# A graph attention layer on one core: GpSimd adds pairs of multiplied rows for VectorE

## Chip, core and metric

One core of a Trainium2 chip runs the whole kernel in one launch. The metric is device time in microseconds (us): the median of the runs shown.

## What is computed

A two-layer graph attention block on 10,000 nodes with 768 numbers each, and 170,000 edges, of which 10,000 are the nodes' own loops. Layer 1 has 4 heads of 256 numbers, layer 2 one head of 768. Cut to what matters here:

```
xl    = (x @ W).reshape(n, heads, out_ch)
e     = leaky_relu(alpha_src[src] + alpha_dst[dst], 0.2)
e     = exp(e - m[dst])                         # m: the largest e of each destination
alpha = e / (s[dst] + 1e-16)                    # s: the sum of e over each destination
msg   = xl[src] * alpha[:, :, None]
out   = segment_sum(msg, dst)                   # one sum of weighted rows for each node
```

The block adds a second edge list of loops to the one given; the kernel takes them in by doubling the weight of row 0. After each layer there is a layer norm and a residual product, and after layer 1 a relu; at the end the input is added and the whole is normalised once more.

## The kernel before

The work has three stages. The first multiplies all nodes by `W1`, writes the products and the attention terms as rows of 1,033 numbers into a table in DRAM, and sorts the nodes by their number of edges. The second is layer 1, the third layer 2. The change is in the second.

Layer 1 goes over 79 tiles of 128 nodes. A tile has as many *rows* as its nodes have edges at most (`SLOTS[t]`, 8 to 41): row k holds, in each partition, the table row of that node's k-th neighbour. The order of the tiles is such that the row counts climb from 8 to 41 and fall again to 9. GpSimd fetches each row by an indirect DMA (`gather`, L426) into a ring of 29 places in SBUF; the place of row k is fetched anew when row k has been used, for the row that comes 29 later. GpSimd works its queue in order, so a gather that waits holds up the next.

For each tile a sum of weighted rows is made in PSUM (`acc`, two of them in turn):

- Rows 0 to 3 (`on_pe`, 4 in every tile of 18 and more rows): ScalarE makes diagonal matrices of the weights (L725), TensorE multiplies and sums (L731).
- Of the others, every fourth (rows 4, 8, 12 and so on) is done by VectorE alone: four instructions that multiply one head and add it to `acc` (L531).
- The three between them are *shared*: ScalarE multiplies the row in place in the ring, one activation for each head (`multiply`, L520), and VectorE adds it to `acc` with one instruction over 1,024 numbers (L527). ScalarE's part is issued `LEAD` = 3 rows ahead (`multiplied(k + 1 + LEAD)`).

The program order within each engine is written out by hand; the loop `for k in range(n)` issues, for each row, ScalarE's multiplication of row k + 3, VectorE's work on row k, the gather into its place (`ring.fetch`), and whatever `due(k)` holds. Among these are the gather of the next tile's input (`next_x`, after row 6), the transposes of the tile before (hT, copied by ScalarE at L698), and its product for layer 2 (L879). Near the end of the loop, at row n - 3, VectorE makes the logits of the next tile (L489 and the lines behind it) from the attention terms in its rows, so these have to have landed by then. Then ScalarE makes the next diagonals. Before the next tile's row 4, VectorE does the layer norm of this one (L542 to L856).

Tiles of 22 and more rows are cut into two or three parts (`cuts_of`). The first part's weights are made ahead, as above; those of a later part are made within the loop (VectorE L489 to L496 and L765 to L773, ScalarE's diagonals L725 and the copy of TensorE's sum L778), and the sum so far is scaled when that part begins (L917).

```
def shared(t, k):
    return by_vector(t, k) and (k - on_pe(t)) % SHARE > 0
```

Of the kernel before, what the change touches and what calls it, by code (L numbers as in the profile page):

```python
# [51 lines left out]
SHARE = 4  # L52
ON_PE1 = 4
PARTED2 = 26
PARTED = 22


def chunk_counts(n_edges):
# [23 lines left out]
def gnn_kernel(ctx, tc, x, x_cols, src, dst, src_col, dst_col, W1, a_src1, a_dst1, b1, g1, be1, Wr1, br1,  # L82
               W2, a_src2, a_dst2, b2, g2, be2, Wr2, br2, out, n_edges):
    nc = tc.nc
# [3 lines left out]
    C1, C2 = H1 * DH1, H2 * DH2  # L88
# [8 lines left out]
    SLOTS = CAPS  # L97
# [3 lines left out]
    FIRST, TOTAL = [0] * NT, 0  # L101
# [414 lines left out]
    def multiply(row, e, dh):  # L516

        for h in range(e.shape[1]):
            s = slice(h * dh, (h + 1) * dh)
            nc.scalar.activation(row[:, s], row[:, s], AF.Copy, scale=e[:, h:h + 1])  # L520
# [13 lines left out]
    def pieces(a, width):  # L534

        return [a[:, c:c + width] for c in range(0, a.shape[1], width)]
# [106 lines left out]
    SLOTS, FIRST = [SLOTS[t] for t in TURNS], [FIRST[t] for t in TURNS]  # L643
# [4 lines left out]
    def begin_layer2(mem):  # L648


        rest = mem.shape[1]

        def at_end(n):
            nonlocal rest
            rest -= n
            return mem[:, rest:rest + n]

        firsts = [(at_end(C1), at_end(D0)) for _ in range(min(2, NT))]
        for t, (hT, xt) in enumerate(firsts):
            nc.sync.dma_start(hT, h1_d[turns[t]])  # L660
            nc.sync.dma_start(xt, x_d[turns[t]])
        wr2 = wr1.rearrange("p k n -> p (k n)")[:, :K1 * C2].rearrange("p (k n) -> p k n", n=C2)
        load(wr2, Wr2)
        br, ones = at_end(C2), at_end(P)
        yield
        nc.vector.memset(ones, 1.0)
        nc.vector.tensor_scalar(br, wr2[:, 0, :], br1_c[:, 0:1], None, op0=OP.mult)
        for k in range(1, K1):
            nc.vector.scalar_tensor_tensor(br, wr2[:, k, :], br1_c[:, k:k + 1], br, op0=OP.mult, op1=OP.add)
        yield wr2, firsts, br, ones, rest  # L670
# [4 lines left out]
    def ordered_layer1(mem):  # L675
        nc.scalar.add_instruction(mybir.InstLoadActFuncSet(name=nc.get_next_instruction_name(), act_func_set_id=6, engine=nc.scalar.engine))
        with tc.tile_pool(name="b1", bufs=1) as pool, tc.tile_pool(name="small1", bufs=2) as small, \
# [3 lines left out]
            ring = Ring(table1, RING1, {}, [mem.rearrange("p (k n) -> p k n", n=R1)])  # L681
# [30 lines left out]
            def on_pe(t):  # L712


                return min(max(SLOTS[t] // 2 - 5, 1), ON_PE1, SLOTS[t])

            def later_on_pe(t):

                return min(max((SLOTS[t] - 20) // 2, 1), ON_PE1)
# [61 lines left out]
            def cuts_of(t):  # L781

                n = SLOTS[t]
                groups = 1 if n < PARTED else -(-2 * n // ring.size)
                size = 8 if groups == 2 else (n - 5) // groups
                return [0] + [n - size * g for g in range(groups - 1, -1, -1)]

            def by_vector(t, k):
                lo = max(c for c in cuts_of(t)[:-1] if c <= k)
                return k - lo >= (later_on_pe(t) if lo else on_pe(t))  # L790

            def shared(t, k):
                return by_vector(t, k) and (k - on_pe(t)) % SHARE > 0
# [22 lines left out]
            for t in range(NT + 1):  # L816
                live, events = t < NT, []
                n = SLOTS[t] if live else 0
                first = done = on_pe(t) if live else 0
                cuts = cuts_of(t) if live else []  # L820
                if live and not ready:
                    ahead = weights_of(t)
                    ready += itertools.islice(ahead, 2)

                def row_of(k):
                    lo = max(c for c in es if c <= k)
                    return es[lo][0][:, k - lo], es[lo][1] if k == lo else None

                def multiplied(upto):
                    nonlocal done  # L830
                    while done < min(upto, n):
                        if shared(t, done):
                            multiply(ring.slot(FIRST[t] + done), row_of(done)[0], DH1)
                        done += 1

                if not live:
                    begin = begin_layer2(mem)
                    next(begin)
                later = iter(())
                if live:  # L840
                    es, acc = ready
                    es, later = dict(es), ahead
                if last:
                    r_before, means = last
                    stats = deviation(small, pieces(means[:, :C1], BANK))
                next(later, None)
                if full is not None:
                    store(t - 2)
                moves = []
                if live and t:  # L850
                    xT, moves = from_x(t)
                multiplied(first + 2)
                if last:
                    h = pool.tile([P, C1], F32, name="h")
                    scaled(h, [means[:, :C1]], stats, g1_b, be1_b)
                    nc.vector.scalar_tensor_tensor(h, h, 0.0, r_before[:, :C1], op0=OP.max, op1=OP.add)  # L856
                if not live:
                    begun = next(begin)
                for move in moves:
                    move()  # L860
                multiplied(first + LEAD)
                if last:
                    hT = pool.tile([P, K1, P], F32, name="hT")
                    events = [(first + j, move) for j, move in enumerate(halves(hT, h))]
                def by_wr1():
                    nonlocal r
                    if live and t:
                        r = product(xT, wr1, C1, ps_r)

                by_wr1()  # L870

                def to_layer2():
                    nonlocal full
                    nc.sync.dma_start(h1_d[t - 1], hT.rearrange("p k n -> p (k n)"))
                    full = []
                    for c in range(0, R2, BANK):
                        q = ps_half.tile([P, BANK], F32, name="half")[:, :min(BANK, R2 - c)]
                        for j in range(K1):
                            nc.tensor.matmul(q, hT[:, j, :], w2[:, j, c:c + q.shape[1]],  # L879
                                             start=(j == 0), stop=(j == K1 - 1))  # L880
                        full.append((c, q))

                if last:
                    events.append((cuts[1] - 2 * LEAD if len(cuts) > 2 else first + 2, to_layer2))

                def next_x():
                    nonlocal xt
                    xt = fetch_x(t + 1)

                if t and t + 1 < NT:  # L890
                    events.append((first + 2, next_x))
                events.sort(key=lambda event: event[0])

                def due(k):
                    while events and events[0][0] <= k:
                        events.pop(0)[1]()

                ready = []
                ahead = iter(())
                if live and t + 1 < NT:  # L900
                    ahead = weights_of(t + 1)
                for k in range(n):
                    if k + 2 * LEAD + 2 in cuts[1:-1]:
                        next(later)
                    if k + 2 * LEAD in cuts[1:-1]:
                        lo, es_lo = next(later)
                        es[lo] = es_lo
                    multiplied(k + 1 + LEAD)
                    if n - LEAD <= k < n - LEAD + 2:
                        ready += itertools.islice(ahead, 1)  # L910
                    if k + 2 in cuts[1:-1]:
                        next(later)
                    weights, fade = row_of(k)
                    if fade is not None:
                        for h in range(H1):
                            s = slice(h * DH1, (h + 1) * DH1)
                            nc.vector.scalar_tensor_tensor(acc[:, s], acc[:, s], fade[:, h:h + 1], ring.slot(FIRST[t] + k)[:, s],  # L917
                                                           op0=OP.mult, op1=OP.add)
                    if by_vector(t, k):
                        weigh(acc, ring.slot(FIRST[t] + k), weights, DH1, shared=shared(t, k))  # L920
                    ring.fetch(FIRST[t] + k + 1 + ring.size)
                    due(k)
                due(DEGREES)
                ready += itertools.islice(ahead, max(2 - len(ready), 0))
                last = None
                if live:
                    last = r, acc
# [459 lines left out]
```

## Time and profile before

| what | value |
|---|---|
| median of 14 runs | 5177.9 us (5174.55 to 5182.29) |
| the profiled execution | 5175.57 us, span 5173.8 us |
| VectorE (DVE) | 4280.8 us busy, 83% of the span |
| TensorE (PE) | 4761.2 us, 92% |
| ScalarE (ACT) | 2818.1 us, 54% |
| GpSimd (POOL) | 3289.0 us, 64% |
| 1500 to 2760 us, the tiles of 18 and more rows | VectorE 1134.70 us busy, TensorE 1135.25, ScalarE 1015.44, GpSimd 834.19 |

The profile names an instruction by its line, engine and operation, then `out<-in` by tile names. Times are microseconds unless marked as nanoseconds. "x12" is twelve instructions merged into one entry; "<-" in square brackets names what ended the idle time before an instruction. A busy TensorE need not be at its peak, since the ends of matmuls are modelled.

### The profile page before, as it was taken

To read this page: it belongs to the slowest core of one execution; us is meant where nothing else is said; L and a number is where in the kernel's file an instruction comes from. 1 tells how busy PE (TensorE), PEld (TensorE's weight loads), DVE (VectorE), ACT (ScalarE), POOL (GpSimd) and SP (SyncE) were. 2 spreads that over 40 slices of the span, in tenths; PEclk is the share of its full clock that TensorE was granted. 3 is DMA by queue.
4 is the path that set the end of the run, shared out by engine and by line. 5 is a ranking of instruction groups with operands and counts; after the bars stand their busy time and mean duration, and the time that the engine had idled before them with its cause. 6 is when DMAs were issued, how large, how long until landed. Compare 5 with 4: busy or idle time off the path is not lost. (4 is left out here: it accounts for less than half of the span.)

```text
span 5173.8 us, 60341 instructions
## 1 busy us (share of the span) xinstructions
PE 4761.2 (92%) x15307; PEld 2861.3 (55%) x15307; DVE 4280.8 (83%) x7678; ACT 2818.1 (54%) x8248; POOL 3289.0 (64%) x3429
## 2 busy tenths in 40 slices
PE   8999998899999988788999999999999999998875
PEld 3444443455555555555555555556666666665554
DVE  4785243899999888889999999789999898888887
ACT  3443433677778787887888777533333333333232
POOL 2445455656666666666666665277777777777774
PEclk9999999999999999999999999999999999999987
DMA  4333533999999999899999999599999999999996
GB/s 160 124 102 87 89 93 123 355 335 353 358 371 371 364 354 350 297 350 353 370 371 366 361 343 336 190 384 358 369 377 377 374 366 364 361 362 362 356 349 217
DMA packets 474312, 1591.43 MB, mean 308 GB/s; under 512 B 118327, under 2 KB 122487, under 8 KB 473958
## 3 DMA queue, kind: packets, MB, share of 16 engines
q0 software_dynamic: 322384, 1286.62, 67.7%
q1 hardware_dynamic: 149520, 297.43, 16.7%
q10 hardware_dynamic: 2054, 3.42, 0.2%
q8 instruction: 129, 2.11, 0.2%
q14 instruction: 225, 1.84, 0.1%
HBM read 1431.80 MB, written 177.29 MB: 311 GB/s over the span
## 5 line engine op out<-in xcount | busy, mean ns | idle before, releaser
L426 POOL DMA_INDIRECT ring<-table,slots x2675 | 2652.2, 991 | 1283.3 <-issue 317.1
L531 DVE SCALAR_TENSOR_TENSOR acc<-ring,e,acc 128x256 f32<-128x256 f32 (+1 forms) x2546 | 1586.5, 623 | 119.9 <-PE acc L731 44.7
L520 ACT ACTIVATE ring<-ring,e 128x256 f32<-128x256 f32 x3232 | 1320.5, 508 | 0.0
L527 DVE TENSOR_TENSOR acc<-acc,ring 128x1024 f32<-128x1024 f32 x808 | 994.9, 1231 | 72.7 <-ACT ring L520 5.6
L173 PE MATMUL big<-w,xT 128*128 128x512 f32 x1896 | 825.4, 597 | 22.9 <-DMA w<-in_W_dram 10.0
L879 PE MATMUL half<-w,hT 128*128 128x512 f32 (+1 forms) x2528 | 830.4, 486 | 0.0
L173 PE MATMUL big<-wr,xT 128*128 128x512 f32 x1896 | 829.5, 594 | 0.2 <-ACT xT L698 0.2
L1033 PE MATMUL big<-wr,w 128*128 128x512 f32 (+1 forms) x2464 | 819.7, 486 | 0.0
L988 PE MATMUL big<-ring,diagonals 128*128 128x256 f32 x2754 | 677.0, 408 | 130.6 <-ACT diagonals L987 111.9
L988 PEld LDWEIGHTS big<-ring,diagonals 128*128 128x128 f32 x2754 | 557.1, 205 | 247.9 <-ACT diagonals L987 149.2
L879 PEld LDWEIGHTS half<-w,hT 128*128 128x128 f32 x2528 | 477.8, 189 | 367.6 <-issue 309.0
L1033 PEld LDWEIGHTS big<-wr,w 128*128 128x128 f32 x2464 | 468.2, 190 | 326.4 <-issue 294.7
L173 PEld LDWEIGHTS big<-w,xT 128*128 128x128 f32 x1896 | 362.0, 192 | 482.0 <-issue 463.6
L731 PE MATMUL acc<-ring,diagonals 128*128 128x256 f32 x2056 | 509.7, 405 | 129.0 <-ACT diagonals L725 120.8
L173 PEld LDWEIGHTS big<-wr,xT 128*128 128x128 f32 x1896 | 355.2, 191 | 417.9 <-issue 417.2
L731 PEld LDWEIGHTS acc<-ring,diagonals 128*128 128x128 f32 x2056 | 411.7, 203 | 223.2 <-ACT diagonals L725 149.5
L987 ACT ACTIVATE diagonals<-ident,e 128x128 f32<-128x128 f32 x1377 | 411.2, 387 | 162.6 <-DVE e L511 134.0
L546 ACT ACTIVATE sd<-mv,eps 128x1 f32<-128x1 f32 x237 | 69.5, 293 | 753.8 <-DVE mv L544 753.7
L630 DVE TENSOR_TENSOR scr<-big,ad_b 128x1024 f32<-128x1024 f32 x79 | 96.7, 1224 | 376.6 <-ACT row L627 376.6
L725 ACT ACTIVATE diagonals<-ident,e 128x128 f32<-128x128 f32 x1028 | 315.2, 388 | 166.3 <-DVE e L511 145.2
L635 POOL TENSOR_TENSOR row<-row,none 128x1024 f32<-128x1024 f32 x79 | 187.1, 2368 | 262.7 <-ACT row L627 262.2
L497 ACT ACTIVATE e<-e 128x32 f32<-128x32 f32 (+26 forms) x174 | 41.1, 236 | 544.2 <-DVE e L496 518.8
(185 smaller groups left out, 3646.9 us busy)
## 6 DMA issues: line engine op xcount, KB each, us to landing
ring<-table,slots POOLq DMA_INDIRECT x2675, 7.0
table<-row SPq DMA_DIRECT2D x79, 516.0 KB, 3.6
h_d<-hT SPq DMA_DIRECT2D x79, 512.0 KB, 6.8
w<-h_d SPq DMA_DIRECT2D x77, 512.0 KB, 8.5
table<-row SPq DMA_DIRECT2D x79, 385.0 KB, 6.0
ring<-table SPq DMA_DIRECT2D x79, 385.0 KB, 6.4
xT<-in_x_cols_dram SPq DMA_DIRECT2D x79, 384.0 KB, 4.4
x_d<-xt SPq DMA_DIRECT2D x79, 384.0 KB, 6.6
```

The source lines that it names most:

```text
L173: nc.tensor.matmul(p[:, c:e], aT[:, j, :], w[:, j, c:e], start=(j == 0), stop=(j == k - 1))
L426: nc.gpsimd.indirect_dma_start(out=to, out_offset=None, in_=table, in_offset=bass.IndirectOffsetOnAxis(ap=index, axis=0), **more)
L520: nc.scalar.activation(row[:, s], row[:, s], AF.Copy, scale=e[:, h:h + 1])
L527: nc.vector.tensor_add(acc[:, :c], acc[:, :c], row[:, :c])
L531: nc.vector.scalar_tensor_tensor(acc[:, s], row[:, s], e[:, h:h + 1], (acc if first is None else first)[:, s], op0=OP.mult, op1=OP.add)
L635: nc.gpsimd.tensor_add(row[:, :C1], row[:, :C1], b1_b)
L725: nc.scalar.activation(diagonals[:, k * H1 + i, :], ident, AF.Copy, scale=e[:, k, i:i + 1])
L731: nc.tensor.matmul(acc[:, c:d], diagonals[:, k * H1 + i, :], ring.slot(q + k)[:, c:d], start=(k == 0 and c % BANK == 0), stop=(k == m - 1 ...
L879: nc.tensor.matmul(q, hT[:, j, :], w2[:, j, c:c + q.shape[1]], start=(j == 0), stop=(j == K1 - 1))
L987: nc.scalar.activation(diagonals[:, (k - lo) % G, :], ident, AF.Copy, scale=e[:, k - lo, :])
L988: nc.tensor.matmul(to, diagonals[:, (k - lo) % G, :], ring.slot(at + k)[:, ON_PE2:C2], start=False, stop=(k == n - 1), skip_group_check=True)
L1033: nc.tensor.matmul(r[:, c:d], hT[:, j, :], wr2[:, j, c:d], start=False, stop=(j == K1 - 1 and d < C2), skip_group_check=True)
```

## The change

In tiles of 18 and more rows (36 of the 79), at row 8 of the loop and ahead of row 8's own gather, GpSimd gets an instruction that adds row 10 to row 11 in place; both are shared rows that ScalarE has multiplied. VectorE's add of row 10 to `acc` is left out, and its add of row 11 takes the sum of the two. No instruction of TensorE, ScalarE or the DMA queue on SyncE is added or removed.

```diff
+PAIRED = 18
...
+            def paired(t):
+
+                return SLOTS[t] >= PAIRED
...
+                    if paired(t) and k == first + SHARE:
+                        one, two = (ring.slot(FIRST[t] + first + SHARE + j)[:, :C1] for j in (2, 3))
+                        nc.gpsimd.tensor_add(two, two, one)
                     weights, fade = row_of(k)
                     if fade is not None:
...
-                    if by_vector(t, k):
+                    if by_vector(t, k) and not (paired(t) and k == first + SHARE + 2):
                         weigh(acc, ring.slot(FIRST[t] + k), weights, DH1, shared=shared(t, k))
                     ring.fetch(FIRST[t] + k + 1 + ring.size)
                     due(k)
```

Here `first` is 4 and `SHARE` is 4.

## Prediction

> **What bounds the kernel now.** I read the page first, then the stretch that holds the 36 paired tiles and VectorE's waits in it, then single tiles in order of time. From the page, the add on each engine (busy us, mean ns | idle before it, and what ended most of it):
>
> ```profile
> L527 DVE TENSOR_TENSOR acc<-acc,ring 128x1024 f32<-128x1024 f32 x808 | 994.9, 1231 | 72.7 <-ACT ring L520 5.6
> L635 POOL TENSOR_TENSOR row<-row,none 128x1024 f32<-128x1024 f32 x79 | 187.1, 2368 | 262.7 <-ACT row L627 262.2
> ```
>
> The same add of 1,024 numbers a partition takes VectorE 1.23 us and GpSimd 2.37. The paired tiles run from 1500 to 2760 us; first their busy times (in the order PE, PE loads, DVE, ACT, POOL, then clock, DMA share, GB/s), then what VectorE waited for:
>
> ```profile
> 1500.00:2760.00 1260.00, 1135.25 (x3818) 701.99 (x3819) 1134.70 (x1814) 1015.44 (x2744) 834.19 (x936) 0.96 0.96 355
> ```
> ```profile
> DVE acc L531 <- PE acc L731: 29.5, 35, 2.3
> DVE acc L527 <- ACT ring L520: 5.1, 5, 1.9
> DVE e L489 <- DMA ring<-table,slots: 4.4, 10, 1.2
> ```
>
> VectorE is busy for 1,135 of 1,260 us and its three largest waits come to 39; the rest is small gaps between its instructions. It sets the pace. TensorE is as busy, but the page puts 120.8 us of idle time before its sums (L731) down to ScalarE's diagonals, so it follows: these come from ScalarE, whose factors come from VectorE's logits near the end of the tile before. DMA is busy too (0.96), yet VectorE waited for rows for only 4.4 us. So 1.23 us taken from VectorE in each tile should count, and so should every new wait of VectorE. What matters is when the sum of rows 10 and 11 is there. A tile of 18 rows, VectorE, ScalarE and GpSimd one after the other:
>
> ```profile
> 1535.12 2.06 DVE L531 SCALAR_TENSOR_TENSOR acc<-ring,e,acc 128x256 f32<-128x256 f32 x4
> 1537.28 3.91 DVE L527 TENSOR_TENSOR acc<-acc,ring 128x1024 f32<-128x1024 f32 x3
> 1541.23 2.06 DVE L531 SCALAR_TENSOR_TENSOR acc<-ring,e,acc 128x256 f32<-128x256 f32 x4
> ```
> ```profile
> 1533.40 1.06 ACT L698 COPY hT<-half 128x512 f32<-128x512 f32 x2
> 1534.34 4.92 ACT L520 ACTIVATE ring<-ring,e 128x256 f32<-128x256 f32 x12
> ```
> ```profile
> 1536.58 0.99 POOL L426 DMA_INDIRECT ring<-table,slots  x1 [0.30 <-issue]
> 1537.87 0.99 POOL L426 DMA_INDIRECT ring<-table,slots  x1 [0.30 <-issue]
> ```
>
> VectorE's three entries are row 8, rows 9 to 11, and row 12. ScalarE's 12 are rows 9, 10 and 11, four heads each (the view ends there): row 11 is multiplied at 1534.34 + 4.92 = 1539.26, after row 9's add has ended (1537.28 + 3.91 / 3 = 1538.6). ScalarE works without a pause here and is ahead of VectorE by only half a row. GpSimd's two are the gathers into the places of rows 7 and 8; the new add stands between them.
>
> **The change, part by part.** *Removed*: 36 adds on VectorE, row 10 of each paired tile, 1.23 us and a gap of 0.1 each: 36 x 1.34 = 48 us off the engine that sets the pace, if nothing takes their place.
>
> *Added*: 36 adds on GpSimd. Each waits for ScalarE's row 11. How soon an engine starts after that, and whether GpSimd's add is slowed by VectorE beside it, is seen in the first stage:
>
> ```profile
> 453.37 1.01 ACT L627 COPY row<-big 128x1024 f32<-128x1024 f32 x1 [5.56 <-issue]
> 454.42 1.22 DVE L630 TENSOR_TENSOR scr<-big,ad_b 128x1024 f32<-128x1024 f32 x1 [4.32 <-ACT row L627]
> 454.47 2.37 POOL L635 TENSOR_TENSOR row<-row,none 128x1024 f32<-128x1024 f32 x1 [1.30 <-ACT row L627]
> ```
>
> GpSimd starts 0.08 us after ScalarE's end (453.37 + 1.01 = 454.38, then 454.47), and takes its usual 2.37 beside a VectorE operation with one operand in PSUM and one in SBUF, which is what rows 8 and 9 are. So in the 18-row tile: the gather before the add ends at 1537.57 and does not bind; the add runs from 1539.34 to 1541.71. VectorE is through with row 9 at 1538.6 and stands for 3.2 us, since row 11 now needs GpSimd. Row 11 then runs from 1541.79 (0.08 again, an estimate from the same row) to 1543.02, where it ended at 1541.19. **The tile is 1.83 us longer, not 1.34 shorter.** Behind the waiting row 11 on VectorE stand rows 12 to 17, the next tile's logits and the layer norm; ScalarE's next diagonals, TensorE's next sums and VectorE's row 4 of the next tile follow from these, so the loss is carried on in full.
>
> I read the same times in each of the 36 tiles. The 24 tiles of 18 to 21 rows: 1.80 to 1.84 in 22 of them, 1.45 in two; together 43.0 us. Four tiles of 22 rows, cut in two parts: 1.30 to 1.38, together 5.4:
>
> ```profile
> 1933.14 1.28 ACT L725 ACTIVATE diagonals<-ident,e 128x128 f32<-128x128 f32 x4
> 1934.31 4.90 ACT L520 ACTIVATE ring<-ring,e 128x256 f32<-128x256 f32 x12
> ```
> ```profile
> 1934.51 3.91 DVE L527 TENSOR_TENSOR acc<-acc,ring 128x1024 f32<-128x1024 f32 x3
> ```
>
> There the diagonals of the second part come first, row 11 is the first of the 12 (4.90 / 3 = 1.63, so 1935.95), and the add ends at 1938.4 against row 9's end at 1935.8. In the eight tiles of 23 and more rows VectorE does the second part's weights between these rows, which covers most of the wait: -0.4 to +2.2, together 4.0. Sum: 43.0 + 5.4 + 4.0 = **+52.4 us**.
>
> *Moved*: on GpSimd's queue the gathers into the places of rows 8 to 11 stand behind the add. In the 18-row tile row 8's is issued at 1542.0 and not at 1537.87: 4.1 later, 2.3 later than VectorE itself has become. Who needs these rows? With a ring of 29, a tile of 18 rows that follows needs none of them before its own last logits were read; in tiles of 19 to 21 the next tile's logits read rows that were gathered just here. An example of 21 rows, row 12's gather and the logits that read it:
>
> ```profile
> 1830.84 0.99 POOL L426 DMA_INDIRECT ring<-table,slots  x1 [0.81 <-DVE acc L531]
> ```
> ```profile
> 1838.27 0.30 DVE L489 TENSOR_TENSOR e<-ring 128x84 f32<-128x84 f32 x1 [0.25 <-DMA ring<-table,slots]
> ```
>
> No slack is left there: the row lands 7.4 us after its issue, and VectorE waits 0.25. The bounds: at worst 17 tiles of 19 to 21 rows x 2.3 = 39 us; at best nothing, because a gather lands 2.1 to 10.5 us after its issue in this stretch (median 7.3), so that part of it is queueing, which a pause of 4 us on the issuing side lets run down. A gain from later gathers is excluded, since nothing starts sooner. I take 8, nearer to nothing, as the queueing above the shortest landing (7.3 - 2.1 = 5.2) is more than the 2.3. GpSimd's own time has room: 834 + 36 x 2.37 = 919 us of busy time in 1,260.
>
> What could lengthen the add is VectorE beside it. The Trainium skill (SBUF — State Buffer, "Who interferes with whom") says that a VectorE instruction with two SBUF inputs contends with a GpSimd instruction that reads SBUF, and that the one that comes second waits out the first. No run shown here has that pair; rows 8 and 9 have one operand in PSUM, so by it only the small weight operations of the eight long tiles could meet the add, at most about 1 us each by an estimate, and the sum would be some 8 us more.
>
> Sum: 52.4 + 8 = 60. The profiled execution took 5175.6 (span 5173.8), so its like would take 5236; the median of the 14 runs lies 2.3 higher at 5177.9, which gives **5238 us**.
>
> **Rivals.** *The gathers come late* (slower still): the same wait, with the 39 in place of the 8: 5178 + 52 + 39 = 5269. For it speaks that the logits of 19 to 21 rows have no slack; against it that a queue empties in a pause.
>
> *The saved add comes out* (faster): VectorE loses 1.34 us a tile and waits for nothing, 5178 - 48 = 5130. It decides at the point where GpSimd's add ends before row 9 does; in the 18-row tile it would have to start by 1538.6 - 2.4 = 1536.2, and ScalarE's row 11 would have to be 3.1 us earlier than it is. ScalarE has no pause in which to catch that up. Even an add that begins as soon as GpSimd is free (1537.6) ends at 1540.0 and brings 0.1 us a tile, or 5174. Three of the long tiles come out faster, by 0.4 at most.
>
> *Something hides the wait* (no change): VectorE already waits 29.5 us for TensorE's first rows, and if those waits were TensorE's own lateness they would shrink by as much; that leaves 52.4 - 29.5 = +23, or 5201, still slower. To reach no change nearly all of the wait must lie beside something else, and nothing of that size is idle on VectorE.
>
> *The change does nothing* is excluded: in the instruction order VectorE has one add fewer and GpSimd one more in each of 36 tiles, and VectorE's row 11 waits for GpSimd in place of ScalarE.
>
> **How the numbers follow.** Forecast, with up to 8 around its terms: 0.80; late gathers 0.11; faster 0.04; wait hidden 0.05, most of it at +23. A difference under 0.2% (10 us) can hardly be told from none here. Faster 0.04, same 0.03, slower 0.93. The range: below, the forecast without the gathers' 8, and half of the 29.5 hidden (5178 + 52 - 15 = 5215); above, the late gathers' 5269 and a little for a GpSimd add that is slower on these rows (0.1 us on 28 tiles is 3): 5272.
>
> **What would show it.** Right: VectorE's row 11 shows a wait for the new GpSimd add of about 3 us in 24 tiles, some 90 us in all; GpSimd's add lasts 2.4 and is released by ScalarE; tile periods of 18 rows grow from 29.8 to 31.6. Wrong: logits that wait for DMA by more than 40 us in all (then the late gathers), an add well over 2.4 us (then contention), or row 11 released by ScalarE or by nothing (then the faster case).

## The result, and the profile after

The changed kernel takes 5240.38 us (median of 6 runs, 5237.59 to 5244.67), the kernel before 5177.24 (28 runs). The ratio is 1.0122, with a 95% interval of 1.0112 to 1.0132: 63 us slower. The profiled execution has a span of 5241.3 us, 67.5 more than before. Lines of code have moved: L426 is now L427, L520 is L521, L527 is L528, L531 is L532, L731 is L736, and the new add is L920.

From the page after, VectorE's add and GpSimd's gathers:

```profile
L427 POOL DMA_INDIRECT ring<-table,slots x2675 | 2646.0, 989 | 1212.1 <-issue 337.1
L528 DVE TENSOR_TENSOR acc<-acc,ring 128x1024 f32<-128x1024 f32 x772 | 950.5, 1231 | 160.7 <-POOL ring L920 94.0
```

The 36 adds are gone (808 to 772, 44 us less busy), and 94.0 us of waiting for the new add stand in their place. The same stretch as before, now up to 2822 us, and VectorE's waits in it:

```profile
1500.00:2822.00 1322.00, 1154.57 (x3826) 718.13 (x3825) 1098.50 (x1775) 1015.65 (x2742) 914.66 (x969) 0.94 0.94 338
```
```profile
DVE acc L528 <- POOL ring L920: 90.8, 30, 3.6
DVE acc L532 <- PE acc L736: 41.0, 36, 2.7
DVE acc L528 <- ACT ring L521: 7.1, 9, 1.9
DVE e L490 <- DMA ring<-table,slots: 4.3, 8, 1.4
```

Two waits have grown by much: that for GpSimd from nothing to 91 us, and row 4's for TensorE from 29.5 to 41.0. The logits' wait for rows has not (4.4 before). The same 18-row tile as before the change, VectorE and then GpSimd, in order of time:

```profile
1539.90 2.06 DVE L532 SCALAR_TENSOR_TENSOR acc<-ring,e,acc 128x256 f32<-128x256 f32 x4
1542.07 1.23 DVE L528 TENSOR_TENSOR acc<-acc,ring 128x1024 f32<-128x1024 f32 x1
1546.51 1.23 DVE L528 TENSOR_TENSOR acc<-acc,ring 128x1024 f32<-128x1024 f32 x1 [3.21 <-POOL ring L920]
```
```profile
1541.37 0.99 POOL L427 DMA_INDIRECT ring<-table,slots  x1 [0.30 <-issue]
1544.12 2.36 POOL L920 TENSOR_TENSOR ring<-ring 128x1024 f32<-128x1024 f32 x1 [1.76 <-ACT ring L521]
1546.63 1.00 POOL L427 DMA_INDIRECT ring<-table,slots  x1 [0.15 <-issue]
```

Row 8, row 9, a wait of 3.21 us, row 11. GpSimd is free at 1542.36, waits 1.76 us for ScalarE's row 11, and adds for 2.36; VectorE goes on 0.03 us after its end. From the start of row 8 to the end of row 11 the tile is 1.77 us longer than before.

Below, *the stretch* is the time from VectorE's row 4 in the first 18-row tile to its row 4 in the first tile behind the paired ones (tile 22 to tile 58 by turn), as the starts in each trace give it: 1274.5 us before, 1339.1 after, 64.6 more.

### The profile page after: what moved, and what is told of

The parts are those of the page before. It is cut to its first block, busy times and chain, and to the rows that moved or that the text cites. A ratio compares the mean times of both kernels' runs of the same rounds, so it can differ in the third digit from the quotient of the medians.

```text
span 5241.3 us, 60307 instructions
## 1 busy us (share of the span) xinstructions
PE 4788.8 (91%) x15307; PEld 2881.4 (55%) x15307; DVE 4246.8 (81%) x7642; ACT 2819.7 (54%) x8248; POOL 3370.6 (64%) x3465
## 3 DMA queue, kind: packets, MB, share of 16 engines
q10 hardware_dynamic: 2054, 3.42, 0.2%
## 5 line engine op out<-in xcount | busy, mean ns | idle before, releaser
L427 POOL DMA_INDIRECT ring<-table,slots x2675 | 2646.0, 989 | 1212.1 <-issue 337.1
L532 DVE SCALAR_TENSOR_TENSOR acc<-ring,e,acc 128x256 f32<-128x256 f32 (+1 forms) x2546 | 1586.5, 623 | 132.1 <-PE acc L736 56.9
L521 ACT ACTIVATE ring<-ring,e 128x256 f32<-128x256 f32 x3232 | 1320.2, 507 | 0.0
L528 DVE TENSOR_TENSOR acc<-acc,ring 128x1024 f32<-128x1024 f32 x772 | 950.5, 1231 | 160.7 <-POOL ring L920 94.0
L736 PE MATMUL acc<-ring,diagonals 128*128 128x256 f32 x2056 | 530.0, 417 | 172.4 <-ACT diagonals L730 143.2
L736 PEld LDWEIGHTS acc<-ring,diagonals 128*128 128x128 f32 x2056 | 427.1, 211 | 271.9 <-ACT diagonals L730 168.2
```

The costliest lines, as they stand in the source:

```text
L427: nc.gpsimd.indirect_dma_start(out=to, out_offset=None, in_=table, in_offset=bass.IndirectOffsetOnAxis(ap=index, axis=0), **more)
L528: nc.vector.tensor_add(acc[:, :c], acc[:, :c], row[:, :c])
L532: nc.vector.scalar_tensor_tensor(acc[:, s], row[:, s], e[:, h:h + 1], (acc if first is None else first)[:, s], op0=OP.mult, op1=OP.add)
L736: nc.tensor.matmul(acc[:, c:d], diagonals[:, k * H1 + i, :], ring.slot(q + k)[:, c:d], start=(k == 0 and c % BANK == 0), stop=(k == m - 1 ...
```

## The experiments

The first eight runs fell on two other chips, on which the kernel before takes 5543 and 5547 us; the changed kernel's traces show where most of that comes from: 1862 us from row 4 of the last tile of layer 1 to the end on the first chip, 2216 on one of these two, but 1339 and 1345 for the stretch. So each run's ratio is to the kernel before on its own chip. The last four ran where it takes 5184. The stretches of the first eight runs have no trace of the kernel before from the same chip beside them, and their one tile of 41 rows took 65 to 73 us where the other traces have 64 to 65; they can be set beside the 1274.5 only to within some 8 us.

| run | ratio to the kernel before, 95% interval | stretch, us |
|---|---|---|
| changed kernel, first chip | 1.0122 (1.0112 to 1.0132) | 1339.1 |
| r1_after_again | 1.0118 (1.0101 to 1.0135) | 1344.7 |
| e1_no_add | 0.9977 (0.9962 to 0.9991) | 1266.2 |
| e2_idle_add, e2b_idle_add | 1.0067 (1.0046 to 1.0087), 1.0054 (1.0037 to 1.0071) | 1318.9, 1316.0 |
| e3_late_take | 1.0082 (1.0064 to 1.0100) | 1314.7 |
| e4_half | 1.0004 (0.9993 to 1.0016) | 1284.6 |
| e5_after_fillers | 1.0087 (1.0066 to 1.0107) | 1333.9 |
| e6_before_fillers | 0.9979 (0.9964 to 0.9994) | 1282.7 |
| r2_before_again | one run, 5188.68 us | 1273.8 |
| e8_fewer_fillers | 0.9991 (0.9982 to 1.0000) | 1266.8 |
| e9_idle_end | 1.0045 (1.0030 to 1.0061) | 1297.5 |
| e10_half_fillers | 0.9994 (0.9985 to 1.0003) | 1271.7 |

**The changed kernel again** (r1_after_again).

> The changed kernel as it is, so that the other runs of this call stand beside it on the same chip. Expected: about 1.012 times the kernel before, as measured first, if the loss is VectorE's wait for GpSimd's add (A), since that wait is set by ScalarE and GpSimd alone. If the loss hangs on when rows land (B), it differs on a chip whose rows land later.

1.0118, the same ratio within the intervals, on a chip whose layer 2 is some 350 us slower. VectorE's wait for GpSimd is again 90.9 us and the logits wait for DMA for 5.9. The loss does not hang on the chip.

**No add at all** (e1_no_add), against the changed kernel:

```diff
-                        nc.gpsimd.tensor_add(two, two, one)
+                        pass
```

> VectorE leaves out row 10 in the 36 tiles and GpSimd adds nothing, so the weighted sums lack row 10. If VectorE alone sets the pace (A), the time falls by 36 x 1.34 = 48 us from the kernel before, to about 5130. If TensorE or the arrival of rows is close behind (B), less comes out: the waits of VectorE's row 4 for TensorE grow and the fall is half or less, 5155 to 5178.

The fall is 12 us (5 to 21 by the interval), not 48 (5530.73 against 5542.73). Tiles of 18 rows, 29.8 us long before, mostly take 29.78. TensorE in one of them, in order of time:

```profile
1542.99 0.82 PE L698 MATMUL half<-ident,xt 128*128 128x128 f32 x6
1544.27 1.09 PE L698 MATMUL half<-ident,h 128*128 128x128 f32 x8 [0.46 <-ACT xT L699]
1545.20 10.47 PE L174 MATMUL big<-wr,xT 128*128 128x512 f32 x24
1555.50 10.51 PE L884 MATMUL half<-w,hT 128*128 128x512 f32 x32
1565.85 7.09 PE L736 MATMUL acc<-ring,diagonals 128*128 128x256 f32 x32
1572.77 0.82 PE L698 MATMUL half<-ident,xt 128*128 128x128 f32 x6
```

Each entry follows on the one before but for 0.46 us: here TensorE has no more time to give. VectorE's row 4 behind these sums waits 1.33 us for them, where it waited 0.66. ScalarE takes its part too. Rows 9 and 11 on VectorE in the same tile, and its waits for ScalarE in the stretch (5.1 us before the change):

```profile
1551.48 1.23 DVE L528 TENSOR_TENSOR acc<-acc,ring 128x1024 f32<-128x1024 f32 x1
1553.45 1.23 DVE L528 TENSOR_TENSOR acc<-acc,ring 128x1024 f32<-128x1024 f32 x1 [0.74 <-ACT ring L521]
```
```profile
DVE acc L528 <- ACT ring L521: 21.4, 24, 6.8
```

Row 11 now comes before ScalarE has multiplied it, so from row 8 to row 11 the 24 tiles of 18 to 21 rows gain 0.7 us each and not 1.34. Even a GpSimd add that cost nothing would have brought about a quarter of what the sum of VectorE's time says.

**An idle add** (e2_idle_add and e2b_idle_add, the same kernel twice), against the changed kernel:

```diff
-                        nc.gpsimd.tensor_add(two, two, one)
+                        idle = pool.tile([P, DH1], F32, name="idle")
+                        for c in range(0, C1, DH1):
+                            nc.gpsimd.tensor_add(idle, two[:, c:c + DH1], one[:, c:c + DH1])
...
-                    if by_vector(t, k) and not (paired(t) and k == first + SHARE + 2):
+                    if by_vector(t, k):
```

> GpSimd makes the same sum at the same place, in four pieces of 256 columns and into a scratch tile that nobody reads; VectorE adds rows 10 and 11 itself as before. If the loss is VectorE's wait for the sum (A), the time is that of the kernel before, 5177 to 5183. If it comes from the gathers that stand behind the add on GpSimd's queue (B), most of it is still there: 5205 or more, with VectorE's logits waiting for DMA.

> The idle add once more, to see whether its +37 us hangs on the chip. By (A) alone it should cost nothing: 0 to +6 us against the kernel before. By (B) it costs 25 us or more and VectorE's logits wait for DMA by 15 us or more in the 36 tiles.

Both came out at half of the whole loss, 37 and 34 us, though VectorE waits for nothing of GpSimd's. What it waits for in the second of them, and GpSimd's groups:

```profile
DVE acc L532 <- PE acc L736: 28.8, 31, 2.5
DVE e L490 <- DMA ring<-table,slots: 19.6, 14, 3.8
```
```profile
L427 POOL DMA_INDIRECT ring<-table,slots x757 | 771.5, 1019 | 321.2 <-issue 186.8 <-DVE acc L532 36.2 <-PE acc L736 31.6
L922 POOL TENSOR_TENSOR idle<-ring 128x256 f32<-128x256 f32 x140 | 102.4, 731 | 19.9 <-issue 6.6 <-ACT ring L521 4.1 <-ACT diagonals L730 0.5
```

The logits wait for rows that were gathered late. In the second run tiles of 18 rows mostly still take 29.8 us; those of 19 and 20 go from 31.2 to 33.2 and from 34.2 to 37.3 in the worst cases, against the first trace of before. GpSimd's gathers wait for themselves ("issue", 187 us against 76 before) and seldom for VectorE (36 against 109 for that line): the queue has become the slow one.

**The sum taken later** (e3_late_take), against the changed kernel; the gathers into places 11 to 13 are issued together after row 13:

```diff
-                    if by_vector(t, k) and not (paired(t) and k == first + SHARE + 2):
+                    if by_vector(t, k) and not (paired(t) and k in (first + SHARE + 2, first + SHARE + 3)):
...
+                    if paired(t) and k == first + SHARE + 5:
+                        weigh(acc, two, weights, DH1, shared=True)
-                    ring.fetch(FIRST[t] + k + 1 + ring.size)
+                    if not (paired(t) and first + SHARE + 3 <= k < first + SHARE + 5):
+                        ring.fetch(FIRST[t] + k + 1 + ring.size)
```

> GpSimd's add stays where it is; VectorE takes the sum after row 13 in place of row 11's turn, so that rows 12 and 13 (2.16 + 1.34 us) lie beside the add, and the gathers into places 11 to 13 follow then. If the place where VectorE takes the sum is what costs (A), VectorE's wait for GpSimd goes below 10 us in all and the time is under that of the kernel before, 5135 to 5165. If the queue behind the add costs (B), the logits of tiles of 19 to 21 rows wait for DMA and the time stays above it, 5185 or more.

VectorE's wait for GpSimd is gone (0.2 us in one case), as was expected; the gain is not. Its waits:

```profile
DVE e L490 <- DMA ring<-table,slots: 37.9, 14, 4.3
DVE acc L532 <- PE acc L736: 33.7, 28, 4.0
```

Late gathers have taken the place of the wait, and a loss of 0.82% is left of 1.18%. Part of this is the edit's own, since it holds the gathers into places 11 and 12 until row 13; how much was not measured. This gives (B) its due: the place where VectorE takes the sum sets what VectorE waits for, not whether it waits.

**The idle add at the end of the tile** (e9_idle_end), against the kernel before:

```diff
                     due(k)
+                    if n >= PAIRED and k == n - 1:
+                        idle = pool.tile([P, DH1], F32, name="idle")
+                        for c in range(0, C1, DH1):
+                            nc.gpsimd.tensor_add(idle, g1_b[:, c:c + DH1], be1_b[:, c:c + DH1])
```

> The idle add of four pieces at the end of each of the 36 tiles, behind the gather of the last row, on constants, so that it waits for nothing. If the idle add cost time by its place, ahead of the gathers into the places of rows 8 to 11 (B), it costs 0 to 8 us here. If it costs by the time that it takes from GpSimd (E), it costs about as much as before, 25 us or more.

It costs 21 us (1.0045), less than (E) expected and more than (B), with no wait in it and nothing but the next gathers behind it. So time taken from GpSimd costs something at this place too. The logits wait for DMA for 19.1 us again. How much of the earlier 34 to 37 us was the place this run does not tell, since its pieces are slower than those were. One tile's pieces on GpSimd, with VectorE's layer norm beside them:

```profile
1752.69 4.04 POOL L927 TENSOR_TENSOR idle<-g,be 128x256 f32<-128x256 f32 x4
1756.87 1.01 POOL L427 DMA_INDIRECT ring<-table,slots  x1
1758.19 1.00 POOL L427 DMA_INDIRECT ring<-table,slots  x1 [0.31 <-PE half L698]
```
```profile
1752.55 1.28 DVE L557 SCALAR_TENSOR_TENSOR h<-acc,mv,g 128x1024 f32<-128x1024 f32 x1
1753.93 1.40 DVE L559 SCALAR_TENSOR_TENSOR h<-h,sd,be 128x1024 f32<-128x1024 f32 x1
1755.44 1.22 DVE L857 SCALAR_TENSOR_TENSOR h<-h,big 128x1024 f32<-128x1024 f32 x1
```

Gathers follow at 1.3 us from one another behind that, 0.30 of it idle. The four pieces take 4.04 us. Three of them last 0.73 to 0.75 us each; the third, which began while L559 ran, lasts 1.59. One such long piece stands in 35 of the 36 tiles. L559 is slower as well, 53.5 us over the stretch against 47.6 for the same line before, so up to 6 of the 21 us are VectorE's own.

**Half an add** (e4_half), against the changed kernel:

```diff
-                        nc.gpsimd.tensor_add(two, two, one)
+                        nc.gpsimd.tensor_add(two[:, :C1 // 2], two[:, :C1 // 2], one[:, :C1 // 2])
...
-                    if by_vector(t, k) and not (paired(t) and k == first + SHARE + 2):
+                    if paired(t) and k == first + SHARE + 2:
+                        nc.vector.tensor_add(acc[:, C1 // 2:C1], acc[:, C1 // 2:C1], one[:, C1 // 2:])
+                    elif by_vector(t, k):
```

> GpSimd adds 512 of the 1,024 columns, VectorE adds the other half of row 10 itself. By A the add is about 1.2 us long (half of 2.36, an estimate) and ends 1.2 us earlier, so a tile of 18 to 21 rows loses 0.6 us and not 1.8: 24 x 0.6 = 14, the long tiles about nothing, in all 5187 to 5197. If an add on GpSimd has a fixed cost or the loss does not hang on its length (B), the time stays above 5215.

The whole loss is gone: 1.0004, better than the 10 to 20 us that were expected by (A). The add takes 1.27 us, and VectorE waits 12.7 us in all for it. An 18-row tile:

```profile
1555.33 1.23 DVE L528 TENSOR_TENSOR acc<-acc,ring 128x1024 f32<-128x1024 f32 x1
1556.67 0.70 DVE L928 TENSOR_TENSOR acc<-acc,ring 128x512 f32<-128x512 f32 x1
1557.93 1.23 DVE L528 TENSOR_TENSOR acc<-acc,ring 128x1024 f32<-128x1024 f32 x1 [0.56 <-POOL ring L920]
```

Row 9 ends at 1556.56 and row 11 begins 1.37 us later; before the change it began 1.44 later. The estimate took ScalarE to end row 11 some 0.7 us after VectorE's row 9, as it did before. In this tile GpSimd's half add began at 1556.62, so ScalarE was through just as row 9 ended: the shift of the engines against each other is not fixed (why it moved was not followed further), and the tile (29.78 us) is TensorE's.

**Fillers for TensorE.** Why does row 4 wait longer for TensorE after the change? A 20-row tile's first sums, before and after (TensorE in order of time):

```profile
2520.50 3.73 PE L731 MATMUL acc<-ring,diagonals 128*128 128x256 f32 x16 [1.43 <-ACT diagonals L725]
```
```profile
2568.95 10.17 PE L736 MATMUL acc<-ring,diagonals 128*128 128x256 f32 x32 [3.25 <-issue]
```

Before, sixteen in 3.73 us behind an idle time of 1.43 (the other sixteen follow, 3.73 again); after, thirty-two in 10.17 behind an idle time of 3.25. The granted clock, in the third column from the right, in windows over these sums after the change, and over the first sixteen before it:

```profile
2569.00:2572.00 3.00, 3.00 (x7) 2.44 (x8) 2.93 (x4) 1.89 (x7) 1.79 (x3) 0.50 1.01 412
2572.00:2575.00 3.00, 3.00 (x8) 2.36 (x7) 2.76 (x4) 2.60 (x10) 1.53 (x2) 0.50 0.81 288
```
```profile
2520.50:2524.00 3.50, 3.50 (x16) 2.95 (x16) 3.33 (x5) 2.02 (x8) 1.84 (x2) 1.00 0.98 361
```

Half the clock after the longer idle time. The Trainium skill (TensorE: Matmul & The Clock Gate, Part 1) states that the array gets half of its clock pulses after about 3.4 us without work, by a window that runs freely, and the full clock again after as long a time of work; these rows agree in kind (0.50 behind 3.25 us, 1.00 behind 1.43), but not with the 3.4. In the same trace of after, the sums at 2639.43 had a clock of 0.58 over their first 3 us behind only 1.94 us of idle time; in the trace of before, those at 2420.26 had 1.00 behind 3.42 us. So the length of the idle time alone does not decide here. Whether the slower clock is what row 4 waits for, fillers in that idle time were to show (e5_after_fillers against the changed kernel; e6_before_fillers puts the same into the kernel before):

```diff
-                        q = ps_half.tile([P, BANK], F32, name="half")[:, :min(BANK, R2 - c)]
+                        whole = ps_half.tile([P, BANK], F32, name="half")
+                        q = whole[:, :min(BANK, R2 - c)]
...
                         full.append((c, q))
+                    if live and 19 <= SLOTS[t] < 38:
+                        bank, fill = whole[:, 258:512], min(4 + 3 * (SLOTS[t] - 19), 10)
+                        for j in range(fill):
+                            nc.tensor.matmul(bank, hT[:, j % K1, :], w2[:, j % K1, :254], start=(j == 0), stop=(j == fill - 1))
```

> The changed kernel, with 4 to 10 more matmuls of 254 columns (4 in tiles of 19 rows, 7 in 20, 10 in 21 and more) behind the product for layer 2 in the tiles of 19 to 27 rows; nobody reads them. They fill TensorE's idle time before the next tile's first sums. If the extra waits of VectorE's row 4 (41 us after against 29.5 before) come from a TensorE that runs slower after an idle time (C), the first sums take 0.38 us in place of 0.63 and the time is 8 to 15 us under that of the changed kernel. If TensorE is late for another reason (D), there is no gain, or a loss where the fillers stand in the way.

> The same fillers in the kernel before, without pairing. VectorE's row 4 waits for TensorE for 0.57 us in most tiles and 0.8 to 2.3 us in the ten where TensorE's first sums are slow; by (C) these ten fall to 0.57, 6 to 10 us in all, and the time is 5168 to 5172 where the kernel before takes 5177. By (D): no change or slower.

With fillers the changed kernel takes 5593.0 us against 5615.24 on the same chip; in the traces the stretch is 10.8 us shorter (4.9 of it in the 41-row tile) and row 4's wait for TensorE goes from 37.4 to 29.6. The two profiled executions differ by 32.8 us, of which 24.7 lie behind layer 1, where nothing was changed; so the 22 us cannot all be put down to the fillers. In the kernel before they bring 0.9979, but its stretch (1282.7) is no shorter than the 1274.5 of the first chip, so that this gain is not shown to be theirs. What decides is the comparison of the two kernels with the same fillers, on one chip: row 4's waits, after and then before the change, differ by 2.1 us where they differed by 11.5 without (41.0 and 29.5, on the first chip).

```profile
DVE acc L532 <- PE acc L736: 29.6, 35, 4.8
```
```profile
DVE acc L532 <- PE acc L736: 27.5, 35, 3.8
```

The granted clock over the paired tiles, 0.96 before and 0.94 after the change, is 0.99 in both of these. And the change now lengthens the stretch by 51.2 us (1333.9 against 1282.7; 54.9 without the 41-row tile) where it was 64.6 (63.9). (C) holds. With fillers only where an idle time stood:

```diff
-                    if live and 19 <= SLOTS[t] < 38:
-                        bank, fill = whole[:, 258:512], min(4 + 3 * (SLOTS[t] - 19), 10)
+                    if live and SLOTS[t] in FILL:
+                        bank, fill = whole[:, 258:512], FILL[SLOTS[t]]
```

> The kernel before with fillers only where TensorE stood idle for 1.4 us and more ahead of its sums: 5 matmuls in tiles of 20 and 21 rows, 10 in 22, 24 and 25, 14 in 23; none in 19, 26 and 27. By (C) the slow first sums go and nothing is put in the way of tiles that had none: 0.2 to 0.4% under the kernel before. By (D): no change or slower.

Row 4's waits for TensorE in the kernel before on this chip (r2_before_again), and with these fillers; the last column is the longest one:

```profile
DVE acc L531 <- PE acc L731: 29.8, 36, 2.1
```
```profile
DVE acc L533 <- PE acc L737: 20.7, 36, 0.7
```

The long waits are all gone, 9.1 us less, and the stretch is 7.0 shorter; the whole time falls by 0.09% (0.9982 to 1.0000), less than the 0.2 to 0.4% expected and hardly clear of the noise.

> The kernel before as it is, for a trace from the chip on which the other runs were made. By every theory: the time of the kernel before on that chip, about 5545 if it is the chip of the last eight runs, with the tiles of 18 rows at 29.8 us each.

That run was for its trace: 5188.68 us, and not the chip of the runs before it, but the stretch (1273.8) and the 18-row tiles (29.8) are those of the first trace.

Half an add with the same fillers (e10_half_fillers):

> GpSimd adds half of the columns, as in the half add (1.0004 times the kernel before), with the same fillers. By (C) the fillers bring the same 0.2 to 0.4% here: 0.996 to 0.999 times the kernel before. If TensorE's slow sums were hidden behind the wait for GpSimd (D), 1.000 or more.

0.9994 (0.9985 to 1.0003): no difference from the kernel before that can be told, and not the 0.996 to 0.999 expected. With half an add GpSimd's help is a wash, with fillers or without. The lowest ratios here are those of the kernel before with fillers, 0.9979 (e6) and 0.9991 (e8), the second at the edge of its interval.

## Why the prediction was right, and where it was not

The forecast was 5238 us, and 5240.4 were measured.

**The wait, its place and its size: right.** Forecast: 1.83 us more for each 18-row tile and 52.4 in all. Over the 36 tiles the time from row 8's start to row 11's end grew by 52.9 us: 41.5 in the 24 tiles of 18 to 21 rows (43.0 forecast), 5.2 in the four of 22 (5.4), 6.1 in the eight longer ones (4.0). The add takes 2.36 us, begins 0.08 behind ScalarE, and VectorE goes on 0.03 after it (0.08 was taken). Periods of 18 rows went from 29.8 to 31.6 as written.

**The 8 us for late gathers: wrong in kind.** The logits' wait for DMA stayed at 4.3 us. What came instead, 11 us by row 4's waits (41.0 against 29.5), was TensorE at half clock, since a later VectorE leaves TensorE idle longer ahead of its sums. The forecast counted TensorE as a follower that only shifts; the fillers show that it also slows, for with them in both kernels 2.1 of the 11.5 us are left. That 8 and 11 lie close together is chance.

**The gathers were not harmless, only covered.** Where VectorE does not wait for the sum, the logits wait for rows (e2, e3, e9). The step "834 + 36 x 2.37 = 919 us in 1,260: room" left out the 0.30 us between one gather and the next, which the profile does not count as busy: with about 790 gathers in the stretch that is 237 us, so by this estimate 1,156 of 1,260 were taken; in a 20-row tile 21 gathers of 1.3, the add and the small operations behind the logits make some 30 us of 32.4 to 34.5.

**The removed add was priced too high.** 48 us "if nothing takes its place" was 12 (e1): "it sets the pace" was read from VectorE's busy time, but TensorE is the bound in tiles of 18 rows, and in those of 18 to 21 ScalarE's row 11 takes half of each saved add away. So the rival "the saved add comes out" had no 5130 to reach. Its 0.1 us a tile for an add that begins as soon as GpSimd is free has the wrong sign besides: with the 0.08 us between the engines row 11 would end at 1541.28, after the 1541.19 of before.

**Contention: not in this change.** L920 took 2346 to 2387 ns on the changed kernel, as GpSimd's add of the first stage did (2346 to 2389), so nothing of the 8 us that the prediction allowed for it came. Where the pair did occur, in e9, the third piece took 1.59 us and not 0.73 beside L559, whose inputs h and be both lie in SBUF, and L559 1.40 and not 1.28. That agrees with the rule of the Trainium skill (SBUF — State Buffer, "Who interferes with whom") named in the prediction.

What stays open: how much of e3's and e9's loss would go if GpSimd's gathers were fewer or shorter, and how the cost of the idle add is shared between its wait, its place and its length; neither was settled.

## What to carry to other kernels

An add given to another engine is worth nothing before its last input is there: read from the trace the moment at which the last input is there and the moment at which the consumer needs the sum, and set what of the helper's own duration does not fit between them against the time saved, however idle the helper looks. Count an engine's queue with the gaps that its instructions bring along, not by its busy share alone. And when one engine falls back, look at what the engine behind it does with the idle time: TensorE here came back at half its clock.

## What was not expected of the hardware

GpSimd's add has a small fixed part: 0.73 us for 256 columns, 1.27 for 512, 2.36 for 1,024. An idle time of 3.25 us ahead of the sums left TensorE at half its granted clock for the next 6 us, and so, for a shorter time, did one of 1.94; one of 1.43 did not, and neither did one of 3.42. Filling such idle times with matmuls that nobody reads shortened VectorE's waits by 9.1 us (e8). A gather issued to GpSimd's queue right behind another holds it for 1.30 us, of which the profile shows 0.99 as busy.
